# Depthwise convolution: the middle kernel column computed by VectorE and ScalarE instead of TensorE

## The chip, the cores and the metric

The kernel runs on one core of a Trainium2 chip. The metric is the device time of one execution in microseconds (us), lower is better. A core has TensorE (PE; its weight loads are listed as PEld), VectorE (DVE), ScalarE (ACT), GpSimd (POOL) and SyncE (SP, which here only issues DMAs). [...]

## What is computed

The input is a batch of 16 images of 56 x 56 pixels with 384 channels, float32. There are two layers. The first is a group normalisation, a dilated attention over 3 x 3 neighbours with dilations 1, 2 and 3, a projection and a residual sum. The second, which the change touches, is a group normalisation, a depthwise 3 x 3 convolution with weights of -1, 0 or 1, and a residual sum:

```python
def _L1_conv_ref(x, w):
    kh, kw, C, mult = w.shape
    w_clip = jnp.clip(w, -1.0, 1.0)
    binary_kernel = w_clip + lax.stop_gradient(jnp.sign(w_clip) - w_clip)
    k = binary_kernel.reshape(kh, kw, 1, C * mult)
    return lax.conv_general_dilated(x, k, window_strides=(1, 1), padding='SAME', rhs_dilation=(1, 1),
                                    dimension_numbers=('NHWC', 'HWIO', 'NHWC'), feature_group_count=C)
...
x = x + _L0_conv_ref(_gn(x), L0_conv_w_qkv, L0_conv_w_proj, L0_conv_b_proj)
x = x + _L1_conv_ref(_gn(x), L1_conv_w)
```

## The kernel before

An image (in the code a block, `b`) is cut into 7 chunks (`c`) of 8 rows, 448 pixels; 112 chunks (`m`) go through three stages. Channels lie on the partitions in 3 groups (`j`) of 128.

Stage A (`plan_a`) loads a chunk, turns it to channels-first on PE, copies it out of PSUM on ACT (`xa`, L435), takes statistics on DVE (L436) and writes it to DRAM (`xd`). Stage B (`plan_b`) is the attention: projections to keys and values (`pkv`) and to queries (`pq`) at L464 on PE, products `t` of queries and keys on DVE (L517), their sums over channels on PE (`ps`, L502), a softmax on DVE, ACT and POOL (L532 to L563), the weights spread over channels on PE (`pb_a`, L581), their products `w` with the values on DVE (L588), sums of these on POOL (L596 to L600), the output projection (`po`, L614), residual sum and statistics on DVE (L617, L620), and a write to DRAM (`x1d`). Stage C (`plan_c`) is the second layer.

In stage C the channel groups 0 and 1 (`JG` = 2 of 3) are convolved on PE. `load` brings three copies `z` of 32 channels, shifted by one row each, onto 96 partitions, `normalise` scales them on ACT (L698), and `convolve` sums over the three rows of the kernel by a matmul with `kdiag`, a 96 x 32 matrix that holds three diagonals of taps, once for each of the three kernel columns (`kx`) and each of the four sets of 32 channels (`q`). The middle column has the full width of 448, the outer two 440 because the edge pixel drops out. Then DVE adds the sum `pc` in PSUM to the residual `x1` (L719; the profile lists that tile as `x`). The third group is convolved elsewhere: on ACT and POOL (`taps_g`, `sum_g`, L770 to L786), in the last block on DVE (`taps_last`, L754). `turn` transposes the result back on PE (`pt_o`, L793), ACT copies it and a DMA writes it out.

The order of the work is written by hand. `at(when, order, piece)` puts a piece in a time slice, nine slices to a chunk (`STEP`), and the number `order` ranks the pieces of one slice (SOFTMAX, SCORE, WEIGH_AHEAD, BURST, STATISTICS, CONVOLVE, WEIGH, QUERY and so on). The pieces are issued in this order; a scheduler then lays the instructions of each engine out by this priority and by what is ready in its own estimate, so the order on the chip deviates from the list in places. In stage C chunk `m` begins at slice `t0` = 9 (m + 10); its two groups are convolved in slices `t0 + 2` and `t0 + 5` (one later where `c` is 0), the residual is loaded at `t0 - 1` and `turn` runs from `t0 + 9`. The last block has denser slices of its own and borrows buffers from stages that are over.

Buffers that matter: `ps_mt`, three PSUM banks, shared by `pkv`, `pt_x`, `pc`, `po`, `pt_s` and `pt_o`; one PSUM buffer each for `pq`, `ps` and for `pb_a` (three banks wide); two `x1`; three `xa`. Group statistics reach stage C as `mr` (shift and scale of each channel, 128 partitions) and `mrz` (the same on the 96 partitions of `z`), from `spread_out`.

Of the kernel before, what the change touches and what calls it, by code (L numbers as in the profile page):

```python
# [35 lines left out]
def dilated_attention_then_binary_conv(  # L36
# [99 lines left out]

    spread = const.tile([P, 2, P], BF16, name="spread")

    ktap = const.tile([P, NTAP], F32, name="ktap")

    kdiag = const.tile([K3, 3, JG * NQ, HD], F32, name="kdiag")

    xin_p = ctx.enter_context(tc.tile_pool(name="xin_p", bufs=1))
    z_p = ctx.enter_context(tc.tile_pool(name="z_p", bufs=2))
    xa_p = ctx.enter_context(tc.tile_pool(name="xa_p", bufs=3))
    st_p = ctx.enter_context(tc.tile_pool(name="st_p", bufs=2))
    dr_p = ctx.enter_context(tc.tile_pool(name="dr_p", bufs=3, space=DRAM))
    xn_p = ctx.enter_context(tc.tile_pool(name="xn_p", bufs=3))
# [6 lines left out]
    x1_p = ctx.enter_context(tc.tile_pool(name="x1_p", bufs=2))  # L155
    xg_p = ctx.enter_context(tc.tile_pool(name="xg_p", bufs=2))
    m_p = ctx.enter_context(tc.tile_pool(name="m_p", bufs=3))
    o_p = ctx.enter_context(tc.tile_pool(name="o_p", bufs=2))


# [34 lines left out]
    def load_small_weights():  # L195

        raw["small"] = t = m_p.tile([P, 3, PX], F32, tag="m", name="small")
        flat = t.rearrange("p k n -> p (k n)")
        at_ = [0]

        def room(parts, n):
            at_[0] += n
            return flat[:parts, at_[0] - n : at_[0]]

        raw["b"] = room(NG, P)
        raw["k"], raw["kp"] = room(K3, 3 * NG * NQ), room(K3, 3 * NG * NQ)
        raw["kg"] = room(P, NTAP)
# [25 lines left out]
    def small_weights():  # L233
# [27 lines left out]

        binary(raw["kp"], raw["k"])
        kp = raw["kp"].rearrange("p (k s) -> p k s", k=3)
        binary(ktap, raw["kg"])
        eye3 = raw["eye"]
        nc.gpsimd.memset(eye3, 0.0)
        for ky in range(3):
# [4 lines left out]
        for kx in range(3):  # L272
            nc.vector.tensor_tensor(
                kdiag[:, kx],
                kp[:, kx, : JG * NQ].unsqueeze(2).to_broadcast([K3, JG * NQ, HD]),
                eye3.unsqueeze(1).to_broadcast([K3, JG * NQ, HD]),
                ALU.mult,
            )
        raw.clear()

    def rows(ap):
        return ap.rearrange("p (r w) -> p r w", w=W)
# [104 lines left out]
    def chunk_of(dram, c):  # L387
        return dram.rearrange("(j p) n -> p j n", p=P)[:, :, c * PX : (c + 1) * PX]
# [7 lines left out]
    stats0, stats1 = {}, {}  # L396
    xd, x1d = {}, {}
    mr0, mr1 = {}, {}
    first = {}
    last_term = {}  # L400

# [44 lines left out]
    def plan_b(m, t0):  # L446
# [198 lines left out]
        for j in range(NG):  # L645
            at(t0 + 24 + j, PROJECT, lambda j=j: out_project(j))

    def plan_c(m, t0):

        b, c = divmod(m, NCH)  # L650
# [38 lines left out]
        def normalise(j):  # L689
# [9 lines left out]
            for edge in edges(j):  # L699
                nc.gpsimd.memset(edge, 0.0)  # L700

        def load_x():
            had["x1"] = x1 = x1_p.tile([P, JG, PX], F32, tag="x1", name="x1")
            nc.sync.dma_start(x1, chunk_of(x1d[b], c)[:, :JG])  # L704

        def convolve(j):
            pc = ps_mt.tile([P, 512], F32, tag="mt", name="pc")
            pcr = rows(pc[:, :PX])

            def tap(kx, q):  # L710
                lo, hi = max(0, 1 - kx), W - max(0, kx - 1)
                return nc.tensor.matmul(  # L712
                    pcr[q * HD : (q + 1) * HD, :, lo:hi], kdiag[:, kx, j * NQ + q, :],
                    rows(set_of(j, q))[:, :, lo + kx - 1 : hi + kx - 1], start=(kx == 1), stop=(kx == 2),
                )
# [3 lines left out]
            nc.vector.tensor_tensor(x1[:, j], pc[:, :PX], x1[:, j], ALU.add)  # L719

        lo, hi = (0 if c else 1), ROWS + (2 if c < NCH - 1 else 1)
        zp = zg[m % 2]

        def load_g():
# [21 lines left out]
        def taps_last(ky):  # L746

            mid = had["xg"][:, 1 : ROWS + 1, :]
            if ky == 0:
                had["m"] = m_p.tile([P, 3, PX], F32, tag="m", name="m")  # L750
            acc = rows(had["m"][:, 0])
            for kx in range(3):
                o = 3 * ky + kx
                nc.vector.scalar_tensor_tensor(  # L754
                    mid if o == 8 else acc, zp[:, ky : ky + ROWS, kx : kx + W], ktap[:, o : o + 1],
                    acc if o else mid, op0=ALU.mult, op1=ALU.add,
                )

# [7 lines left out]
        def taps_g(ky):  # L766
            t = m_p.tile([P, 3, PX], F32, tag="m", name="m")
            for kx in range(3):
                o = 3 * ky + kx
                nc.scalar.activation(  # L770
                    rows(t[:, kx]), zp[:, ky : ky + ROWS, kx : kx + W], AF.Copy, scale=ktap[:, o : o + 1]
                )
# [15 lines left out]
        def turn(s):  # L788
            pt = ps_mt.tile([P, 512], F32, tag="mt", name="pt_o")
            mid = had["xg"][:, 1 : ROWS + 1, :].rearrange("p r w -> p (r w)")  # L790
            for j in range(NG):
                src = mid if j == JG else had["x1"][:, j]
# [10 lines left out]
        if b == B - 1:  # L803
# [54 lines left out]
    def statistics(when, sets):  # L858
# [3 lines left out]
        def norm(k, *which):  # L862
            if not steps:
                steps["of"] = group_norm([
                    (stats1[b], lambda mr, mrz, b=b: mr1.update({b: (mr, mrz)}), True) if layer
                    else (stats0[b], lambda mr, b=b: mr0.update({b: mr}), False)
                    for layer, b in sets
                ])
            steps["of"][k](*which)
# [49 lines left out]
```

## Time and profile before

| quantity | value |
|---|---|
| median of 3 runs | 5223.8 us (5223.65 to 5231.6) |
| the profiled execution | 5223.35 us, its span 5221.6 us |
| mean granted TensorE clock | 0.984 |
| L712, all matmuls of the convolution | 5040 with `z` in, 336 with `z_last` (the last block) |
| L588, `w` on DVE | 1008, 1560.3 us busy |
| L517, `t` on DVE | 1008, 1528.6 us busy |
| L596, sums of `w` on POOL | 672, 2048.7 us busy |
| L770, taps of the third group on ACT | 945, 658 ns each |
| DVE waiting for `pc` at L719 | 239.3 us |
| PE waiting for `w` at `pb_a` | 36.7 us |
| DMA, mean | 158 GB/s, 825.62 MB |

A line of groups reads: line of the code, engine, operation, output <- input, shapes, count, then busy time, mean length of one in ns, and the idle time of that engine right before it with what ended it. A line of the timeline reads: start, length, engine, line, operation, and in brackets the idle time before it. A float32 matmul appears as two records in the trace. Times in the text that look like 2083.95 are microseconds from the start of the span.

### The profile page before, as it was taken

To read this page: it belongs to the slowest core of one execution; us is meant where nothing else is said; L and a number is where in the kernel's file an instruction comes from. 1 tells how busy PE (TensorE), PEld (TensorE's weight loads), DVE (VectorE), ACT (ScalarE), POOL (GpSimd) and SP (SyncE) were. 2 spreads that over 40 slices of the span, in tenths; PEclk is the share of its full clock that TensorE was granted. 3 is DMA by queue.
4 is the path that set the end of the run, shared out by engine and by line. 5 is a ranking of instruction groups with operands and counts; after the bars stand their busy time and mean duration, and the time that the engine had idled before them with its cause. 6 is when DMAs were issued, how large, how long until landed. Compare 5 with 4: busy or idle time off the path is not lost. (4 is left out here: it accounts for less than half of the span.)

```text
span 5221.6 us, 75614 instructions
## 1 busy us (share of the span) xinstructions
PE 5085.7 (97%) x26885; PEld 2322.5 (44%) x26885; DVE 4199.0 (80%) x4125; ACT 2310.7 (44%) x4077; POOL 4242.2 (81%) x2950
## 2 busy tenths in 40 slices
PE   8999999999999999999999999999999999999976
PEld 4444444444444444444444444444444444444433
DVE  4898888888888888888888888888888888878764
ACT  3223444444444544444444444444445444444444
POOL 2677878888888888889888888888888888888881
PEclk8999999999999999999999999999999999999987
DMA  6444656666566565656666565665666656554445
GB/s 197 127 124 119 167 160 166 163 166 167 162 169 165 161 163 159 168 158 166 166 166 165 163 166 162 165 163 160 164 163 171 167 163 168 141 138 135 121 135 158
DMA packets 811631, 825.62 MB, mean 158 GB/s; under 512 B 360307, under 2 KB 801014, under 8 KB 811254
## 3 DMA queue, kind: packets, MB, share of 16 engines
q1 hardware_dynamic: 803270, 808.79, 56.9%
q10 hardware_dynamic: 7984, 12.00, 0.7%
q8 instruction: 213, 3.49, 0.3%
q14 instruction: 164, 1.34, 0.1%
HBM read 466.41 MB, written 231.21 MB: 134 GB/s over the span
## 5 line engine op out<-in xcount | busy, mean ns | idle before, releaser
L596 POOL TENSOR_TENSOR w<-w 128x1344 f32<-128x1344 f32 x672 | 2048.7, 3049 | 327.3 <-DVE w L588 279.1
L517 DVE TENSOR_TENSOR t<-pq,k 128x1344 f32<-128x1344 f32 x1008 | 1528.6, 1550 | 237.8 <-PE pq L464 236.6
L588 DVE TENSOR_TENSOR w<-pb_a,v 128x1344 f32<-128x1344 f32 x1008 | 1560.3, 1548 | 172.6 <-PE pb_a L581 91.9
L464 PE MATMUL pkv<-xn,wqkvT 128*128 128x448 f32 x3924 | 1542.2, 542 | 3.9 <-ACT xa L435 3.5
L464 PEld LDWEIGHTS pkv<-xn,wqkvT 128*128 128x128 f32 x3924 | 725.9, 190 | 664.7 <-issue 634.7
L614 PE MATMUL po<-y,wprojT 128*128 128x448 f32 x2016 | 834.9, 550 | 17.3 <-POOL y L600 17.3
L464 PE MATMUL pq<-xn,wqkvT 128*128 128x448 f32 x1962 | 834.9, 560 | 0.0
L698 ACT ACTIVATE z<-z,mrz 96x448 f32<-96x448 f32 x840 | 573.9, 751 | 266.0 <-DMA z<-x1d 239.7
L777 POOL TENSOR_TENSOR m<-m 128x1344 f32<-128x1344 f32 x210 | 639.1, 3044 | 43.3 <-ACT m L770 37.9
L502 PE MATMUL ps<-t,sel 128*32 128x448 f32 x6048 | 660.8, 546 | 0.3 <-DVE t L517 0.2
L474 ACT COPY v<-pkv 128x448 f32<-128x448 f32 x336 | 178.1, 530 | 918.3 <-PE pkv L464 911.1
L770 ACT ACTIVATE m<-zg,ktap 128x448 f32<-128x448 f32 x945 | 552.6, 658 | 15.1 <-POOL m L777 5.7
L614 PEld LDWEIGHTS po<-y,wprojT 128*128 128x128 f32 x2016 | 376.1, 191 | 374.1 <-issue 347.1
L712 PE MATMUL pc<-z,kdiag 96*32 96x440 f32 (+1 forms) x5040 | 519.3, 545 | 7.1 <-POOL z L700 4.3
L464 PEld LDWEIGHTS pq<-xn,wqkvT 128*128 128x128 f32 x1962 | 345.2, 190 | 318.8 <-issue 318.8
L617 DVE SCALAR_TENSOR_TENSOR xr<-po,bias,xr 128x448 f32<-128x448 f32 x336 | 227.9, 678 | 277.8 <-PE po L614 272.7
L435 ACT COPY xa<-pt_x 128x448 f32<-128x448 f32 x315 | 167.4, 534 | 618.2 <-PE pt_x L423 618.2
L558 POOL TENSOR_TENSOR rest<-ew,e 112x512 f32<-112x512 f32 x112 | 130.1, 1162 | 358.9 <-ACT e L554 358.9
L581 PE MATMUL pb_a<-aT,spread 24*128 24x448 bf16 x3024 | 369.5, 360 | 42.7 <-DVE w L588 36.7
L600 POOL TENSOR_TENSOR y<-y,w 128x448 f32<-128x448 f32 x336 | 381.7, 1136 | 23.8
L599 POOL TENSOR_TENSOR y<-w 128x448 f32<-128x448 f32 x336 | 382.8, 1139 | 19.3
L581 PEld LDWEIGHTS <-spread 24*128 24x128 bf16 x3024 | 100.8, 91 | 621.4 <-issue 603.6
(132 smaller groups left out, 4307.6 us busy)
## 6 DMA issues: line engine op xcount, KB each, us to landing
z<-x1d SPq DMA_DIRECT2D x570, 224.0 KB, 4.0
xr<-xd SPq DMA_DIRECT2D x112, 672.0 KB, 4.3
x1d<-xr SPq DMA_DIRECT2D x112, 672.0 KB, 3.2
xn<-xd SPq DMA_DIRECT2D x109, 672.0 KB, 4.5
xin<-in_x_dram SPq DMA_DIRECT2D x105, 672.0 KB, 7.3
xd<-xa SPq DMA_DIRECT2D x315, 224.0 KB, 3.2
out_dram<-osb SPq DMA_DIRECT2D x420, 168.0 KB, 3.4
x<-x1d SPq DMA_DIRECT2D x112, 448.0 KB, 8.5
```

What stands on the lines that cost most here:

```text
L464: nc.tensor.matmul(dst[:, :PX], wqkvT[:, cc, o0 : o0 + P], had["xn"][:, cc, :], start=(cc == 0), stop=(cc == NG - 1))
L502: return nc.tensor.matmul(had["ps"][32 * j : 32 * j + 32, :PX], sel[:, s0 : s0 + 32], tk, start=(issued[j] == 1), stop=(issued[j] == len(r ...
L517: nc.vector.tensor_tensor(t.rearrange("p k (r w) -> p k r w", w=W), q3, k3, ALU.mult)
L581: return nc.tensor.matmul(pb[:, kx, :PX].rearrange("p (s n) -> p s n", s=NSUB), spread[rows_of, v % 2, :], had["a"][rows_of, :, v // 8, :] ...
L588: nc.vector.tensor_tensor(w.rearrange("p k (r w) -> p k r w", w=W), pb[:, :, :PX].rearrange("p k (r w) -> p k r w", w=W), three(kv[1][g][m ...
L596: nc.gpsimd.tensor_tensor(w0, w0, w, ALU.add)
L599: nc.gpsimd.tensor_tensor(y, w0[:, 0], w0[:, 1], ALU.add)
L614: nc.tensor.matmul(po[:, :PX], wprojT[:, g, j * P : (j + 1) * P], had[f"y{g}"], start=(g == 0), stop=(g == NG - 1))
L698: nc.scalar.activation(z, z, AF.Identity, bias=mrz[:, j, q, 0:1], scale=mrz[:, j, q, 1:2])
L712: return nc.tensor.matmul(pcr[q * HD : (q + 1) * HD, :, lo:hi], kdiag[:, kx, j * NQ + q, :], rows(set_of(j, q))[:, :, lo + kx - 1 : hi + k ...
L770: nc.scalar.activation(rows(t[:, kx]), zp[:, ky : ky + ROWS, kx : kx + W], AF.Copy, scale=ktap[:, o : o + 1])
L777: nc.gpsimd.tensor_tensor(had["m"], had["m"], t, ALU.add)
```

## The change

The middle column (`kx` = 1) of the groups 0 and 1 is no longer a matmul. With the normalisation of a channel written as scale and shift, its three taps act on the raw residual `x1`: above, centre and below, each times (tap x scale), plus a constant (sum of the taps in range x shift). `column_scalars` computes these factors once a block on POOL, adding 1 to the centre's so that the residual sum is in it. For each group `column` computes the centre and the constant on ACT into a new buffer `u` (one, of 448 elements), in the first or last chunk of an image in two instructions, because the border row has another constant. In `convolve` PE adds up the two outer columns, DVE then adds the taps above and below into `pc` in PSUM by two multiply-adds, and the last add takes `u` in place of `x1`.

`load_x` brings ten rows in place of eight and is placed at `t0 - 4`, ahead of `load(0)` in that slice. `column` is placed in the slice of its `convolve`, at the rank STATISTICS, ahead of CONVOLVE; in the last block it has the rank CONVOLVE itself. At the start the taps of all three groups are loaded to `ktap` by three DMAs in place of one. `xa` has two buffers in place of three, and the small tile `sm` of the softmax shares the buffer of `mx`. The three buffers of `m_p`, which hold the last block's products, are as before.

```diff
-    xa_p = ctx.enter_context(tc.tile_pool(name="xa_p", bufs=3))
+    xa_p = ctx.enter_context(tc.tile_pool(name="xa_p", bufs=2))
...
+    u_p = ctx.enter_context(tc.tile_pool(name="u_p", bufs=1))
...
-        nc.sync.dma_start(raw["kg"], w_conv.rearrange("y x c m -> c (y x m)")[JG * P : (JG + 1) * P, :])
+        for j in range(NG):
+            nc.sync.dma_start(
+                raw["kg"][:, j * NTAP : (j + 1) * NTAP],
+                w_conv.rearrange("y x c m -> c (y x m)")[j * P : (j + 1) * P, :],
+            )
...
+        up, mid, down = (ktap[:, :JG, o] for o in (1, 4, 7))
+        nc.vector.tensor_add(kcol[:, :, 0], mid, down)
+        nc.vector.tensor_add(kcol[:, :, 1], kcol[:, :, 0], up)
+        nc.vector.tensor_add(kcol[:, :, 2], up, mid)
...
-            sm = s_p.tile([SUB, NSUB, GH], F32, tag="sm", name="sm")
+            sm = s_p.tile([SUB, NSUB, GH], F32, tag="mx", name="sm")
...
+    def column_scalars(b):
+
+        mr = mr1[b][0]
+        cs = st_p.tile([P, JG, 6], F32, tag="cs", name="cs")
+        nc.gpsimd.tensor_tensor(
+            cs[:, :, 0:3], ktap[:, :JG, 1:NTAP:3], mr[:, :JG, 1:2].to_broadcast([P, JG, 3]), ALU.mult
+        )
+        nc.gpsimd.tensor_tensor(cs[:, :, 3:6], kcol, mr[:, :JG, 0:1].to_broadcast([P, JG, 3]), ALU.mult)
+        nc.gpsimd.tensor_scalar(cs[:, :, 1], cs[:, :, 1], 1.0, None, op0=ALU.add)
+        cs1[b] = cs
...
         def load_x():
-            had["x1"] = x1 = x1_p.tile([P, JG, PX], F32, tag="x1", name="x1")
-            nc.sync.dma_start(x1, chunk_of(x1d[b], c)[:, :JG])
+            had["x1"] = x1 = x1_p.tile([P, JG, ROWS + 2, W], F32, tag="x1", name="x1")
+            nc.sync.dma_start(
+                x1[:, :, lo:hi, :].rearrange("p j r w -> p j (r w)"),
+                x1d[b].rearrange("(j p) n -> p j n", p=P)[:, :JG, p0 + (lo - 1) * W : p0 + (hi - 1) * W],
+            )
+
+        def column(j):
+
+            x1, cs = had["x1"], cs1[b]
+            had["u"] = u = u_p.tile([P, ROWS, W], F32, tag="u", name="u")
+            parts = [(0, 1, 3), (1, ROWS, 4)] if c == 0 else [(0, ROWS, 4)]
+            if c == NCH - 1:
+                parts = [(0, ROWS - 1, 4), (ROWS - 1, ROWS, 5)]
+            for r0, r1, of in parts:
+                nc.scalar.activation(
+                    u[:, r0:r1], x1[:, j, r0 + 1 : r1 + 1], AF.Identity, bias=cs[:, j, of : of + 1], scale=cs[:, j, 1:2]
+                )
...
-            in_one_go([lambda kx=kx, q=q: tap(kx, q) for kx in (1, 0, 2) for q in (3, 0, 1, 2)])
-            x1 = had["x1"]
-            nc.vector.tensor_tensor(x1[:, j], pc[:, :PX], x1[:, j], ALU.add)
+            in_one_go([lambda kx=kx, q=q: tap(kx, q) for kx in (0, 2) for q in (3, 0, 1, 2)])
+            x1 = had["x1"][:, j]
+            mid = x1[:, 1 : ROWS + 1]
+            cs, above, below = cs1[b], 1 if c == 0 else 0, ROWS - 1 if c == NCH - 1 else ROWS
+            nc.vector.scalar_tensor_tensor(
+                pcr[:, above:], x1[:, above:ROWS], cs[:, j, 0:1], pcr[:, above:], op0=ALU.mult, op1=ALU.add
+            )
+            nc.vector.scalar_tensor_tensor(
+                pcr[:, :below], x1[:, 2 : below + 2], cs[:, j, 2:3], pcr[:, :below], op0=ALU.mult, op1=ALU.add
+            )
+            nc.vector.tensor_tensor(mid, pcr, had["u"], ALU.add)
...
+                at(t0 + 1 + j, CONVOLVE, lambda j=j: column(j))
                 at(t0 + 1 + j, CONVOLVE, lambda j=j: convolve(j))
...
-        at(t0 - 1, LOADS, load_x)
+        at(t0 - 4, LOADS, load_x)
         for j in range(JG):
             at(t0 - 4 + 3 * j, LOADS, lambda j=j: load(j))
+            at(t0 + 2 + 3 * j + late, STATISTICS, lambda j=j: column(j))
             at(t0 - 1 + 3 * j + late, NORM, lambda j=j: normalise(j))
             at(t0 + 2 + 3 * j + late, CONVOLVE, lambda j=j: convolve(j))
```

More of the change, by code (lines that the diff above doesn't have):

```diff
@@ L137, in dilated_attention_then_binary_conv @@
     spread = const.tile([P, 2, P], BF16, name="spread")
-    ktap = const.tile([P, NTAP], F32, name="ktap")
-    kdiag = const.tile([K3, 3, JG * NQ, HD], F32, name="kdiag")
+    ktap = const.tile([P, NG, NTAP], F32, name="ktap")
+    kcol = const.tile([P, JG, 3], F32, name="kcol")
+    kdiag = const.tile([K3, 2, JG * NQ, HD], F32, name="kdiag")
     xin_p = ctx.enter_context(tc.tile_pool(name="xin_p", bufs=1))
     z_p = ctx.enter_context(tc.tile_pool(name="z_p", bufs=2))
-    xa_p = ctx.enter_context(tc.tile_pool(name="xa_p", bufs=3))
+    xa_p = ctx.enter_context(tc.tile_pool(name="xa_p", bufs=2))
     st_p = ctx.enter_context(tc.tile_pool(name="st_p", bufs=2))
@@ L206, in load_small_weights @@
         raw["k"], raw["kp"] = room(K3, 3 * NG * NQ), room(K3, 3 * NG * NQ)
-        raw["kg"] = room(P, NTAP)
+        raw["kg"] = room(P, NG * NTAP)
         raw["eye"] = room(K3, HD)
@@ L263, in small_weights @@
         kp = raw["kp"].rearrange("p (k s) -> p k s", k=3)
-        binary(ktap, raw["kg"])
+        binary(ktap.rearrange("p j o -> p (j o)"), raw["kg"])
+        up, mid, down = (ktap[:, :JG, o] for o in (1, 4, 7))
+        nc.vector.tensor_add(kcol[:, :, 0], mid, down)
+        nc.vector.tensor_add(kcol[:, :, 1], kcol[:, :, 0], up)
+        nc.vector.tensor_add(kcol[:, :, 2], up, mid)
         eye3 = raw["eye"]
@@ L271, in small_weights @@
             )
-        for kx in range(3):
+        for kx in (0, 2):
             nc.vector.tensor_tensor(
-                kdiag[:, kx],
+                kdiag[:, kx // 2],
                 kp[:, kx, : JG * NQ].unsqueeze(2).to_broadcast([K3, JG * NQ, HD]),
@@ L398, in dilated_attention_then_binary_conv @@
     mr0, mr1 = {}, {}
+    cs1 = {}
     first = {}
@@ L700, in normalise @@
                 nc.gpsimd.memset(edge, 0.0)
+        lo, hi = (0 if c else 1), ROWS + (2 if c < NCH - 1 else 1)
         def load_x():
-            had["x1"] = x1 = x1_p.tile([P, JG, PX], F32, tag="x1", name="x1")
-            nc.sync.dma_start(x1, chunk_of(x1d[b], c)[:, :JG])
+            had["x1"] = x1 = x1_p.tile([P, JG, ROWS + 2, W], F32, tag="x1", name="x1")
[13 more added lines that the diff above has]
+                )
         def convolve(j):
@@ L710, in tap @@
             def tap(kx, q):
-                lo, hi = max(0, 1 - kx), W - max(0, kx - 1)
+                x0, x1 = max(0, 1 - kx), W - max(0, kx - 1)
                 return nc.tensor.matmul(
-                    pcr[q * HD : (q + 1) * HD, :, lo:hi], kdiag[:, kx, j * NQ + q, :],
-                    rows(set_of(j, q))[:, :, lo + kx - 1 : hi + kx - 1], start=(kx == 1), stop=(kx == 2),
-                )
-            in_one_go([lambda kx=kx, q=q: tap(kx, q) for kx in (1, 0, 2) for q in (3, 0, 1, 2)])
-            x1 = had["x1"]
-            nc.vector.tensor_tensor(x1[:, j], pc[:, :PX], x1[:, j], ALU.add)
-        lo, hi = (0 if c else 1), ROWS + (2 if c < NCH - 1 else 1)
+                    pcr[q * HD : (q + 1) * HD, :, x0:x1], kdiag[:, kx // 2, j * NQ + q, :],
+                    rows(set_of(j, q))[:, :, x0 + kx - 1 : x1 + kx - 1], start=(kx == 0), stop=(kx == 2),
+                    skip_group_check=True,
+                )
+            in_one_go([lambda kx=kx, q=q: tap(kx, q) for kx in (0, 2) for q in (3, 0, 1, 2)])
[9 more added lines that the diff above has]
+            nc.vector.tensor_tensor(mid, pcr, had["u"], ALU.add)
         zp = zg[m % 2]
@@ L754, in taps_last @@
                 nc.vector.scalar_tensor_tensor(
-                    mid if o == 8 else acc, zp[:, ky : ky + ROWS, kx : kx + W], ktap[:, o : o + 1],
+                    mid if o == 8 else acc, zp[:, ky : ky + ROWS, kx : kx + W], ktap[:, JG, o : o + 1],
                     acc if o else mid, op0=ALU.mult, op1=ALU.add,
@@ L770, in taps_g @@
                 nc.scalar.activation(
-                    rows(t[:, kx]), zp[:, ky : ky + ROWS, kx : kx + W], AF.Copy, scale=ktap[:, o : o + 1]
+                    rows(t[:, kx]), zp[:, ky : ky + ROWS, kx : kx + W], AF.Copy, scale=ktap[:, JG, o : o + 1]
                 )
@@ L791, in turn @@
             for j in range(NG):
-                src = mid if j == JG else had["x1"][:, j]
+                src = mid if j == JG else had["x1"][:, j, 1 : ROWS + 1].rearrange("p r w -> p (r w)")
                 nc.tensor.transpose(pt[:SUB, j * P : (j + 1) * P], src[:, s * SUB : (s + 1) * SUB], ident)
@@ L864, in norm @@
                 steps["of"] = group_norm([
-                    (stats1[b], lambda mr, mrz, b=b: mr1.update({b: (mr, mrz)}), True) if layer
+                    (stats1[b], lambda mr, mrz, b=b: (mr1.update({b: (mr, mrz)}), column_scalars(b)), True) if layer
                     else (stats0[b], lambda mr, b=b: mr0.update({b: mr}), False)
```

## The prediction

> **What bounds the kernel now.** I read the page's table of busy time first, then the busy time by stretches, then the groups of instructions by shape, and last one chunk in order of time on TensorE (PE) and VectorE (DVE).
>
> ```profile
> PE 5085.7 (97%) x26885; PEld 2322.5 (44%) x26885; DVE 4199.0 (80%) x4125; ACT 2310.7 (44%) x4077; POOL 4242.2 (81%) x2950
> 200.00:400.00 200.00, 200.00 (x867) 88.25 (x866) 181.05 (x169) 44.28 (x79) 145.17 (x89) 1.00 0.47 133
> 500.00:4800.00 4300.00, 4272.47 (x22833) 1945.47 (x22831) 3538.65 (x3413) 2001.25 (x3533) 3660.72 (x2414) 1.00 0.60 162
> ```
>
> In the second and third line the columns are the stretch, its length, then busy time of PE, PEld, DVE, ACT, POOL, the granted clock, DMA share and GB/s. From 500 to 4800 us PE is idle for 27.5 us in 4300, at full clock: PE is the bound, and any PE time taken out can be gained until somebody else is late. DVE is busy 82%, POOL 85%, ACT 47%. The stretch from 200 to 400 us, before any convolution runs, shows something useful: there DVE is busy 90.5% and PE still never idles.
>
> ```profile
> L712 PE MATMUL pc<-z,kdiag 96*32 96x440 f32 x3360 | 355.3, 541 | 0.0
> L712 PE MATMUL pc<-z,kdiag 96*32 96x448 f32 x1680 | 202.7, 554 | 7.1 <-POOL z L700 4.3 <-ACT z L698 2.5 <-DVE x L719 0.3
> L719 DVE TENSOR_TENSOR x<-pc,x 128x448 f32<-128x448 f32 x224 | 139.4, 622 | 241.6 <-PE pc L712 239.3 <-DMA x<-x1d 2.3
> L617 DVE SCALAR_TENSOR_TENSOR xr<-po,bias,xr 128x448 f32<-128x448 f32 x336 | 227.9, 678 | 277.8 <-PE po L614 272.7
> ```
>
> The 448-wide row is the middle column, the 440-wide one the two outer ones. L719 empties the convolution today: DVE reaches it early and waits 239.3 us for PE over the run.
>
> ```profile
> 2075.32 0.60 DVE L538 TENSOR_REDUCE mx<-pt_s 112x48 f32<-112x432 f32 x1
> ...
> 2082.42 1.53 DVE L588 TENSOR_TENSOR w<-pb_a,v 128x1344 f32<-128x1344 f32 x1
> 2084.38 0.62 DVE L719 TENSOR_TENSOR x<-pc,x 128x448 f32<-128x448 f32 x1 [0.43 <-PE pc L712]
> 2084.92 1.55 DVE L588 TENSOR_TENSOR w<-pb_a,v 128x1344 f32<-128x1344 f32 x1
> 2087.10 1.56 DVE L517 TENSOR_TENSOR t<-pq,k 128x1344 f32<-128x1344 f32 x1 [0.63 <-PE pq L464]
> ...
> 2090.57 3.00 DVE L517 TENSOR_TENSOR t<-pq,k 128x1344 f32<-128x1344 f32 x2
> ```
>
> ```profile
> 2081.90 2.41 PE L712 MATMUL pc<-z,kdiag 96*32 96x448 f32 x24
> 2084.25 0.36 PE L581 MATMUL pb_a<-aT,spread 24*128 24x448 bf16 x3
> 2084.54 2.52 PE L464 MATMUL pq<-xn,wqkvT 128*128 128x448 f32 x6
> 2086.99 0.36 PE L581 MATMUL pb_a<-aT,spread 24*128 24x448 bf16 x3
> ...
> 2093.83 1.71 PE L502 MATMUL ps<-t,sel 128*32 128x448 f32 x16
> ```
>
> This is the tight part of an ordinary chunk: DVE works without a pause from 2071.79 (softmax, products `t`, `w`) to 2083.95, and its only idle time before `t` ends at 2093.57 is 0.43 + 0.63 = 1.06 us. The score burst `ps` starts 0.26 us after that `t`. Later in the chunk DVE waits 2.28 us for `po`.
>
> **What the Trainium skill says.** TensorE: Matmul & The Clock Gate, Part 3 (packing): matmuls whose outputs lie in different 32-partition column tiles run at the same time. The trace agrees: 24 matmuls of about 0.54 us end within 2.41 us. VectorE: DVE Perf Modes, the perf-mode tier table: an fp32 operand in PSUM keeps an operation at one element a cycle; the trace agrees (L588 against L719: 926 ns for 896 more elements, 1.03 ns each). SBUF — State Buffer, Who interferes with whom: a VectorE instruction with two SBUF inputs contends with a GpSimd one that reads SBUF, one with a single SBUF input does not. The trace agrees: L546, two SBUF inputs, takes 0.609 us at the median and 3.362 at most; L617, PSUM and SBUF, never exceeds 0.685. The new multiply-adds are of L617's kind. PSUM — Partial Sum Buffer, The four PSUM rules: the first matmul of a group clears written-marks for its bank and quadrants, and a later one overwrites where a mark is clear. So the edge column that only the third tap column writes comes out right without the middle one; no run here shows it yet.
>
> **The change part by part.**
>
> *PE, removed.* One of three tap columns: 8 of the 24 matmuls in 2.44 us (the usual length of L712 in the timeline), 0.81 us a channel group, two groups: 1.63 us a chunk. 105 chunks outside the last block: 171 us. In the last block the clock is about 0.7 and the two groups take 8 us, so 2.7 us a chunk less, which is treated below.
>
> *DVE, added.* Two multiply-adds per group, PSUM and SBUF in, PSUM out. No row of before writes PSUM from DVE. Below: 0.61, the pitch at which an L617 lets the next operation start. Above: if reading and writing the same PSUM tile do not overlap, 0.62 + 448 x 1.03 ns = 1.08, taken as 1.15. I take 0.70, the pitch of the chained multiply-adds of L754 at the end of the run: +1.4 us a group, +2.8 a chunk. The add that remains is today's L719 with `u` for `x1`. DVE goes from 3538.65/96 = 36.9 us a chunk (96 softmaxes in the stretch) to 39.7; PE from 44.5 to 42.9. That is 92.5% of PE, a little above the 90.5% at which PE did not idle.
>
> *What is queued behind them.* The new operations wait for `pc`, with a `w` and a `t` behind them on DVE; `pb_a` has one buffer, so PE waits for that `w`. Keeping the order above: `pc` ends at 2083.5, but PE's next `pb_a` waits for the `w` that ends at 2083.95, and `pq` behind it ends at 2086.7. DVE is free at 2083.95 too: the three convolution steps end at 2085.95, the next `w` at 2087.4. So PE stands until 2087.4 at the `pb_a` that was at 2086.99: 0.4 late instead of 0.81 early, and `ps` with it (its `t` ends at 2093.57 - 1.06 + 1.4 = 2093.9 and does not hold it longer). The second group (`pc` at 2095.76) then gives its 0.81 back, and DVE catches up in the pause before `po`. By this walk only 0.4 us of 1.63 remain a chunk. Against it: the order is laid out again for the new costs, and PE has projections ready that need nothing of DVE; 200 to 400 us shows that it finds them. I let an ordinary chunk give back 0.33 us (about a quarter of the walk's 1.23), bounds 0 and 1.23.
>
> *Chunks with statistics*, 15 in the steady part: DVE has 2.6 us more there (L345, 2.63 at the median, behind a POOL sum), and already stalls PE by 1.42 us at 2007.95. I take 1.1 of 1.63 given back, bounds 0 and 2.5.
>
> *ScalarE.* `column`: 224 activations like L770 at 0.66, 150 us over the run; ACT reaches 50%. It waits for `x1`, which is asked for three slices sooner, and stands ahead of its matmuls; 0. Without that cover (x1 late) evictions of `pkv` queue behind it; the DMA lands in 8.5 us and six slices of about 5 us are left. Bounds 0 and 0.2 a chunk.
>
> *POOL.* Three small operations a block, about 0.2 us each: 10 us over the run, plus a wait for `mr` with sums behind it. 0, bounds 0 and 1 us a block.
>
> *SP and DMA.* `load_x` takes ten rows for eight, 112 KB more a chunk (12.5 MB on 825.6), and passes ahead of the first `z` load on SP; already today it is issued at 2096.66, before `z` at 2098.26. ACT waits 239.7 us for `z` in all, but that `z` is multiplied some 12 us later. 0, bounds 0 and 0.3. Two `xa` buffers for three: a turn every two slices, landing 3.2 us: 0. The shared softmax tag: `mx` is read out before `sm` is written: 0.
>
> *Start.* Two more tap loads of 1152 small elements (today's one landed in 10.6 us, while DMA is full to 40 us) and some small DVE operations: +3 us, bounds 0 and 10.
>
> *Last block.* About 13.4 us a chunk. DVE is in the ring: L719 at 5185.79, six tap sums to 5190.52, `z_last`, and PE starts at 5191.12. PE loses 2.7 us a chunk; DVE, 8.5 us of work in it, gains 2.8 and ends later behind each `pc`. Taken as 0, bounds -12 and +12 for seven chunks.
>
> *Sum.* -171 + 90 x 0.33 (30) + 15 x 1.1 (17) + 3 = -121. From the profiled execution's 5223.35 us (span 5221.6): 5102. The median of the runs shown, 5223.8, is 0.45 us off, nothing here.
>
> **Rivals.**
> A, as summed: 5102, with 0.1 to 0.9 us given back its own range is 5075 to 5155. Chance 0.45.
> B, PE stays full: nothing given back, 5055. For it: 200 to 400 us. Against: DVE at 92.5% and POOL at 38.1/42.9 = 89% together, where POOL had only 73% in that stretch. 0.17.
> C, the walk holds: 90 x 0.4 - 3 = 33 us, 5190. For it: no pause on DVE from 2071.79 to 2083.95. 0.15.
> N, the returns eat just what is saved, within 0.2%: 0.05.
> D, slower: the in-place multiply-adds cost 1.15 us. DVE gains 2.3 us before `w` in each group; in the walk that exceeds its pause of 1.06 plus the 0.81 that comes back later by 0.43. 90 x 0.43 + 15 x 1 + 3 = +57: 5280. It decides from about 0.94 us each on. For it: no row shows DVE writing PSUM. Against: DVE would still have 41.5 us of work for 42.9. 0.18.
> That the computation differs (edge column) would not change the time.
>
> **How the numbers follow.** Forecast 5102. A and B and C are faster: 0.77; same 0.05 (0.2%, about 10 us, is what a measurement of this kernel can tell from no change); slower 0.18. The range leaves out D's upper part and B's lower edge: 5040 to 5230. A's own range stands above.
>
> **What would show it.** Right: PE about 98% in 500 to 4800 with L712 at two thirds of its matmuls; DVE 91 to 93%; the new lines at 0.6 to 0.75 us; more waits of `pb_a` for `w` than today's 36.7 us, some 50. Wrong: multiply-adds over 0.9 us (D); `pb_a` waiting over 100 us (C); PE over 99% (B); ACT waiting for `x1`, or a last block over 10 us longer.

## Result and profile after

| kernel | median (lowest to highest), runs | ratio to before |
|---|---|---|
| before | 5226.58 us (5223.65 to 5231.6), 4 | |
| after | 5152.15 us (5150.29 to 5160.07), 4 | 0.9867, 95% interval 0.9855 to 0.9879 |

The change makes the kernel 1.3% faster. The forecast was 5102 us, 121 us below the profiled execution of before. The profiled execution of after took 5160.07 us, 63 below it; it is the slowest of its four, and by the medians the change gives 74. So between a half and two thirds of what was forecast arrived. The rest of this text asks where the other part is.

First the page's table of busy time of the kernel after, then its stretch from 500 to 4700 us (columns as in the prediction: stretch, length, busy time of PE, PEld, DVE, ACT and POOL, clock, DMA share, GB/s):

```profile
PE 4967.5 (96%) x25093; PEld 2259.1 (44%) x25093; DVE 4475.9 (87%) x4575; ACT 2478.8 (48%) x4365; POOL 4248.0 (82%) x2998
```

```profile
500.00:4700.00 4200.00, 4143.10 (x21157) 1881.54 (x21157) 3749.61 (x3774) 2126.96 (x3747) 3639.68 (x2437) 1.00 0.61 167
```

PE is still the bound, with 56.9 us of pauses in 4200 (1.35%; 0.6% before), and DVE is busy 89%, where 91 to 93 was forecast. It has more to do, but the chunk is longer than forecast. The groups by shape of the kernel after:

```profile
L762 DVE SCALAR_TENSOR_TENSOR pc<-x,cs,pc 128x448 f32<-128x448 f32 x192 | 131.9, 687 | 119.5 <-PE pc L752 93.1 <-issue 15.6 <-DMA x<-x1d 4.9
L765 DVE SCALAR_TENSOR_TENSOR pc<-x,cs,pc 128x448 f32<-128x448 f32 x192 | 131.0, 683 | 2.8
L768 DVE TENSOR_TENSOR x<-pc,u 128x448 f32<-128x448 f32 x224 | 137.7, 615 | 2.0 <-ACT u L742 0.2
L752 PE MATMUL pc<-z,kdiag 96*32 96x440 f32 x3360 | 359.5, 546 | 8.8 <-POOL z L723 7.6 <-ACT z L721 0.6 <-ACT osb L846 0.5
```

The first two lines are the new multiply-adds, 0.687 and 0.683 us each, never over 0.691; 0.70 was taken. The last line is what is left of the convolution on PE, 3360 of 5040 matmul records.

To see where the time went, take the sum of the softmax (L544 before, L556 after), which DVE computes once in each chunk; the distance from one to the next is the length of a chunk. Such marks, read from the timelines of both kernels, divide the span:

| stretch | before, us | after, us | difference |
|---|---|---|---|
| start to the 11th softmax sum (no convolution yet) | 507.5 | 515.5 | +8.0 |
| 11th to 101st | 4037.9 | 3963.5 | -74.5 |
| 101st to the last (112th) | 487.2 | 493.0 | +5.8 |
| last one to the end (the last block's convolution) | 189.0 | 186.0 | -3.1 |

Within an image an ordinary chunk goes from 44.1 to 43.4 us. The chunk with the statistics goes from 48.3 to 46.8, the one after it from 44.9 to 43.4, the next mostly from 44.1 to 44.1.

So the steady part gains only 0.7 us in an ordinary chunk. On the timeline of PE, `pc` at L752 keeps PE for 0.75 us less in each group (1.66 for 2.41), 1.5 us a chunk in all. About half of that is lost again inside the chunk. The timeline of PE in the kernel before, with the projections behind the transposes:

```profile
2087.29 0.60 PE L423 MATMUL pt_x<-ident,xin 112*128 112x112 f32 x4
2087.73 0.39 PE L793 MATMUL pt_o<-ident,x 128*112 128x128 f32 x2
2087.95 0.27 PE L793 MATMUL pt_o<-ident,xg 128*112 128x128 f32 x1
2088.06 4.68 PE L464 MATMUL pkv<-xn,wqkvT 128*128 128x448 f32 x12
```

and the same place in the kernel after:

```profile
2541.78 1.66 PE L752 MATMUL pc<-z,kdiag 96*32 96x440 f32 x16
...
2546.42 0.60 PE L435 MATMUL pt_x<-ident,xin 112*128 112x112 f32 x4
2546.86 0.38 PE L841 MATMUL pt_o<-ident,x 128*112 128x128 f32 x2
2547.08 0.27 PE L841 MATMUL pt_o<-ident,xg 128*112 128x128 f32 x1
2547.64 4.78 PE L476 MATMUL pkv<-xn,wqkvT 128*128 128x448 f32 x12 [0.29 <-ACT xa L447]
```

Before, the first `pkv` starts 0.11 us behind the last transpose; after, 0.56 us, behind a wait for ACT's eviction of `pt_x` into `xa`. A projection needs no `xa`. What it needs is a bank: `pc`, `pt_x`, `pt_o` and `pkv` share the three banks of `ps_mt`. The timeline of DVE in the same stretch of after shows who holds one:

```profile
2543.51 0.69 DVE L762 SCALAR_TENSOR_TENSOR pc<-x,cs,pc 128x448 f32<-128x448 f32 x1 [1.00 <-PE pc L752]
2544.11 1.55 DVE L600 TENSOR_TENSOR w<-pb_a,v 128x1344 f32<-128x1344 f32 x1
2545.57 0.68 DVE L765 SCALAR_TENSOR_TENSOR pc<-x,cs,pc 128x448 f32<-128x448 f32 x1
2546.23 1.56 DVE L529 TENSOR_TENSOR t<-pq,k 128x1344 f32<-128x1344 f32 x1
2547.70 0.61 DVE L768 TENSOR_TENSOR x<-pc,u 128x448 f32<-128x448 f32 x1
```

DVE now has three operations on `pc`, and between them stand a `w` and a `t`. So `pc` keeps its bank from 2541.78 to 2548.31, 6.5 us; before it was 3.1 us, from 2081.90 to 2085.00. When PE comes to `pkv`, the bank of `pc` is not free and `pt_o` has only just been written; by the releaser, it gets the bank of `pt_x`. The evictions of `pt_x` by ACT in these two places, before and after, agree:

```profile
2087.93 0.53 ACT L435 COPY xa<-pt_x 128x448 f32<-128x448 f32 x1 [4.90 <-PE pt_x L423]
2547.06 0.53 ACT L447 COPY xa<-pt_x 128x448 f32<-128x448 f32 x1 [5.72 <-PE pt_x L435]
```

Before, `pkv` starts 0.40 us ahead of the end of this eviction (2088.46), so it had the other bank, that of `pc`, free since 2085.00. After, it starts 0.05 us behind that end (2547.59), with `pc` still to be emptied until 2548.31.

The waits of the whole run, kernel after (waiting engine and line, releaser, then us in all, times, the longest):

```profile
PE pb_a L593 <- DVE w L600: 48.4, 47, 2.5
PE pkv L476 <- ACT xa L447: 26.2, 78, 3.5
PEld pkv L476 <- ACT xa L447: 45.8, 78, 4.2
```

and of the kernel before:

```profile
PE pb_a L581 <- DVE w L588: 36.7, 31, 2.4
PEld pkv L464 <- ACT xa L435: 6.4, 12, 0.5
PE pkv L464 <- ACT xa L435: 3.5, 12, 0.3
```

The wait that the prediction watched, `pb_a` for `w`, grew by 11.7 us over the run, and the wait of `pkv` for `xa` went from 12 places to 78. These are my two theories. The first is **the held bank**: the added work costs nothing as such, and the time is lost because `pc` keeps one of three banks for twice as long. Its rival is **the load**: DVE has 2.8 us more to do in a chunk, `w` comes later for it, and PE waits at `pb_a` or for what follows.

### The profile page after: what moved, and what is told of

Same layout as the page of the kernel before. It is cut to its first block, busy times and chain, and to the rows that moved or that the text cites. A ratio compares the mean times of both kernels' runs of the same rounds, so it can differ in the third digit from the quotient of the medians.

```text
span 5157.9 us, 72661 instructions
## 1 busy us (share of the span) xinstructions
PE 4967.5 (96%) x25093; PEld 2259.1 (44%) x25093; DVE 4475.9 (87%) x4575; ACT 2478.8 (48%) x4365; POOL 4248.0 (82%) x2998
## 5 line engine op out<-in xcount | busy, mean ns | idle before, releaser
L476 PE MATMUL pq<-xn,wqkvT 128*128 128x448 f32 x1962 | 862.4, 567 | 0.0
L818 ACT ACTIVATE m<-zg,ktap 128x448 f32<-128x448 f32 x945 | 568.9, 659 | 17.6 <-POOL m L825 8.5
L593 PE MATMUL pb_a<-aT,spread 24*128 24x448 bf16 x3024 | 370.4, 360 | 52.6 <-DVE w L600 48.4
L629 DVE SCALAR_TENSOR_TENSOR xr<-po,bias,xr 128x448 f32<-128x448 f32 x336 | 227.5, 677 | 210.7 <-PE po L626 205.8
L752 PE MATMUL pc<-z,kdiag 96*32 96x440 f32 x3360 | 359.5, 546 | 8.8 <-POOL z L723 7.6
```

The source lines that it names most:

```text
L476: nc.tensor.matmul(dst[:, :PX], wqkvT[:, cc, o0 : o0 + P], had["xn"][:, cc, :], start=(cc == 0), stop=(cc == NG - 1))
L593: return nc.tensor.matmul(pb[:, kx, :PX].rearrange("p (s n) -> p s n", s=NSUB), spread[rows_of, v % 2, :], had["a"][rows_of, :, v // 8, :] ...
L752: return nc.tensor.matmul(pcr[q * HD : (q + 1) * HD, :, x0:x1], kdiag[:, kx // 2, j * NQ + q, :], rows(set_of(j, q))[:, :, x0 + kx - 1 : x ...
L818: nc.scalar.activation(rows(t[:, kx]), zp[:, ky : ky + ROWS, kx : kx + W], AF.Copy, scale=ktap[:, JG, o : o + 1])
```

## The experiments

All ratios are to the kernel before on the same chip, with a 95% interval. The lengths of chunks and the stretches are those of the profiled execution.

**One part of the change at a time.** `pe_only` leaves out the three taps of the middle column altogether:

```diff
-            nc.vector.scalar_tensor_tensor(
-                pcr[:, above:], x1[:, above:ROWS], cs[:, j, 0:1], pcr[:, above:], op0=ALU.mult, op1=ALU.add
-            )
...
-            nc.vector.tensor_tensor(mid, pcr, had["u"], ALU.add)
+            nc.vector.tensor_tensor(mid, pcr, mid, ALU.add)
...
-            at(t0 + 2 + 3 * j + late, STATISTICS, lambda j=j: column(j))
```

> Leaves out all three taps of the middle kernel column (no u, no multiply-adds; the last add takes x1), so that only the PE part of the change remains. Bank theory (the new kernel keeps only half of the PE time it saves because pc stays in one of the three shared PSUM banks for 6.5 us a group instead of 3.1): pc is short-lived again, so the whole saving shows, 1.52 us a chunk, an ordinary chunk of 42.6 us and 5065 to 5080 us in all. Load theory (VectorE is 89% busy and late with w): the same, since its work is gone too. If the chunk stays near 43.4 us, PE itself loses the time and both theories fall.

Measured: 5111.9 us, ratio 0.9791 (0.9776 to 0.9805), ordinary chunk 42.8 us: 32 us above the range that both theories had set, and 0.2 above their chunk. Where these 0.2 are is seen below, side by side with the others. `dve_only` is the other part alone: all the added work of DVE, ACT and POOL, with the middle column left on PE as well (by the first column's taps) and so counted in two places:

```diff
-                    rows(set_of(j, q))[:, :, x0 + kx - 1 : x1 + kx - 1], start=(kx == 0), stop=(kx == 2),
+                    rows(set_of(j, q))[:, :, x0 + kx - 1 : x1 + kx - 1], start=(kx == 1), stop=(kx == 2),
...
-            in_one_go([lambda kx=kx, q=q: tap(kx, q) for kx in (0, 2) for q in (3, 0, 1, 2)])
+            in_one_go([lambda kx=kx, q=q: tap(kx, q) for kx in (1, 0, 2) for q in (3, 0, 1, 2)])
```

> Puts the middle column back on PE beside the new work on VectorE and ScalarE (that column is counted twice, with the first column's taps). If what is given back is a fixed price of the new work, the two parts add up: this run less before equals the new kernel less the one with the PE part alone, about +75 to +85 us, 5300 us. If the new work hides behind a longer PE, it is 5230 to 5250, of which about 8 at the start. Bank theory: PE waits of pkv for the eviction of xa about as many as in the new kernel (78). Load theory: fewer waits of any kind than in the new kernel.

Measured: 5281.5 us, 1.0115 (1.01 to 1.013), ordinary chunk 44.7, 0.6 above before; the total lies between the two ranges of the expectation. The two parts nearly add up: the ordinary chunk loses 1.3 us by the one and gains 0.6 by the other, and 0.7 net is what after shows. Both theories can live with that. But the waits of `dve_only` lean to the bank:

```profile
PEld pkv L476 <- ACT xa L447: 44.8, 78, 3.5
PE pb_a L593 <- DVE w L600: 33.5, 29, 2.5
PE pkv L476 <- ACT xa L447: 25.2, 78, 2.7
```

With all the added work of DVE, PE waits no more for `w` than before (36.7 us in 31 places), and for the bank as often as in after.

**The bank freed sooner.** `add_first` keeps all the work. It only issues the next `t` on DVE behind the addition that frees `pc`:

```diff
+    def behind_add(what):
+        if what not in add_of[1]:
+            return nullcontext()
+        add_of[1].discard(what)
+        return tc.issue_after(add_of[0].ins)
...
-            nc.vector.tensor_tensor(t.rearrange("p k (r w) -> p k r w", w=W), q3, k3, ALU.mult)
+            with behind_add("t"):
+                nc.vector.tensor_tensor(t.rearrange("p k (r w) -> p k r w", w=W), q3, k3, ALU.mult)
...
-            nc.vector.tensor_tensor(mid, pcr, had["u"], ALU.add)
+            add_of[0] = nc.vector.tensor_tensor(mid, pcr, had["u"], ALU.add)
+            add_of[1] = {"w", "t"}
```

> Only the order on VectorE: the next score product t is issued behind the add that frees pc, instead of between the second multiply-add and that add. Bank theory: pc of the first group is free some 1.5 us sooner, pkv no longer waits for xa (0.45 us a chunk, 78 waits), an ordinary chunk falls from 43.4 to about 42.9, 5110 to 5125 us in all. Load theory: VectorE has the same work, chunk 43.4, 5145 to 5160.

Measured: 5093.27 us, 0.9754 (0.9739 to 0.9768), some 58 us below after and 17 below the range of the bank theory, ordinary chunk 42.7. `pkv` waits for `xa` in 13 places, where it was 78 in after. DVE in the timeline of `add_first`:

```profile
2518.31 0.69 DVE L771 SCALAR_TENSOR_TENSOR pc<-x,cs,pc 128x448 f32<-128x448 f32 x1 [0.21 <-PE pc L761]
2518.91 1.55 DVE L609 TENSOR_TENSOR w<-pb_a,v 128x1344 f32<-128x1344 f32 x1
2520.38 0.68 DVE L774 SCALAR_TENSOR_TENSOR pc<-x,cs,pc 128x448 f32<-128x448 f32 x1
2521.09 0.62 DVE L777 TENSOR_TENSOR x<-pc,u 128x448 f32<-128x448 f32 x1
```

and PE:

```profile
2516.58 1.66 PE L761 MATMUL pc<-z,kdiag 96*32 96x440 f32 x16
...
2521.88 0.27 PE L851 MATMUL pt_o<-ident,xg 128*112 128x128 f32 x1
2521.99 4.68 PE L484 MATMUL pkv<-xn,wqkvT 128*128 128x448 f32 x12
```

The addition ends at 2521.71, before the last transpose, and `pkv` starts 0.11 us behind that transpose again, without a wait. All of DVE's added work is still there, and its busy share from 500 to 4700 us rises to 91%. With all of it the kernel is faster than `pe_only`, which does none of it. So the load is not what after loses. (`pe_only` is no lower bound, because leaving operations out also lays the order out anew: there PE waits 59.2 us at `pb_a` for `w`, here 37.0.)

**The same wait brought into the kernel before.** `hold_before` takes the kernel before, with no work added, and puts the addition behind the next `t` (the last eleven chunks keep the old order):

```diff
-            nc.vector.tensor_tensor(t.rearrange("p k (r w) -> p k r w", w=W), q3, k3, ALU.mult)
+            product = nc.vector.tensor_tensor(t.rearrange("p k (r w) -> p k r w", w=W), q3, k3, ALU.mult)
...
+            if late_add:
+                with tc.issue_after(product.ins):
+                    late_add.pop()()
...
-            nc.vector.tensor_tensor(x1[:, j], pc[:, :PX], x1[:, j], ALU.add)
+            late_add.append(lambda: nc.vector.tensor_tensor(x1[:, j], pc[:, :PX], x1[:, j], ALU.add))
+            if b == B - 1 or m > N - 12:
+                late_add.pop()()
```

> The kernel before the change, with the one addition that frees the bank of pc issued behind the next score product t; no work added or taken away. If it is the time for which pc keeps its bank that costs, the projections wait for the eviction into xa in some 78 places, an ordinary chunk goes from 44.1 to 44.6 us or so, and the time is 5255 to 5275. If it is VectorE's added work, this order costs nothing: 5221, chunk 44.1.

Measured: 5294.36 us, 1.0136 (1.0122 to 1.015), ordinary chunk 44.7, the length of `dve_only` without any of its work. PE in the timeline of `hold_before`:

```profile
2481.65 0.27 PE L799 MATMUL pt_o<-ident,xg 128*112 128x128 f32 x1
2482.21 4.78 PE L465 MATMUL pkv<-xn,wqkvT 128*128 128x448 f32 x12 [0.29 <-ACT xa L436]
```

It is the picture of after to the hundredth: 0.56 us from transpose to projection, 0.29 of it the wait for `xa`. `pkv` waits for `xa` in 65 places and for `osb`, the eviction of `pt_o`, in 14 more. DVE in the same stretch:

```profile
2480.80 1.56 DVE L518 TENSOR_TENSOR t<-pq,k 128x1344 f32<-128x1344 f32 x1 [0.81 <-PE pq L465]
2484.27 0.61 DVE L723 TENSOR_TENSOR x<-pc,x 128x448 f32<-128x448 f32 x1
```

`pc` was complete at 2478.01. DVE stands for 0.81 us ahead of this `t` and does not take the addition in the meantime: it keeps the order of its queue, in which a `w` and a statistics operation follow before the addition.

The total is 19 us above the expected range, since the chunks with statistics became 49.4, 51.1 or 52.8 us long (48.3 before), where I had expected an ordinary chunk's loss. In those of 51.1 us the granted clock is at half once for 3.4 us, in those of 52.8 twice, in those of 49.4 never; the last section comes back to that.

The smaller number of `xa` buffers is not why `pkv` waits for `xa`: `hold_before` has three of them, and the kernel before with two (`before_xa2`, below) waits in 12 places, as before.

**The order alone, and the work with the order.** Two controls: `before_add_first` is the kernel before with `t` behind its addition, `dve_first` is `dve_only` with it. Both edits are those of `add_first`.

> The kernel before the change with the next score product t behind the addition that frees the bank, nothing else. There pc keeps its bank for 3.1 us already: the order has little to give, 5215 to 5223 us and a chunk of 44.1. If the order is worth something for itself, whatever the change does, the kernel before gains as much as the changed one did from it (57 us): about 5165.

Measured: 5223.88 us, 1.0 (0.9991 to 1.0009), ordinary chunk 44.1. This control says less than it was meant to: between the 21st and the 101st softmax sum of the kernel before, no `t` stands between a complete `pc` and its addition in any of the 160 groups, so there the edit had nothing to move.

> The kernel dve_only (all three columns on TensorE, the middle one counted twice over by the added VectorE and ScalarE work) with the next score product t behind the addition that frees the bank. If the held bank is the whole of what the added work costs, an ordinary chunk is back at 44.1 to 44.2 us and the time at 5221 to 5230 (5 us of it from the start). If VectorE's added 2.8 us a chunk cost something for themselves, the chunk stays above 44.4 and the time above 5245.

Measured: 5254.56 us, 1.0059 (1.0042 to 1.0076): in time on the side of the load, though the ordinary chunk is 44.3 us, just over the bank's 44.2. The stretches show why. Against before it has +9.1 us up to the 11th softmax sum, +14.6 in the 90 chunks of the steady part (`dve_only`: +42.6), -5.5 up to the last sum, and +15.9 from there to the end. The last is the block whose convolution nothing else covers: with all three columns on PE the added work does cost time there, 15 us in `dve_only` too. I had left it out of this expectation.

Side by side, with the time from the first matmul of `pc` to the end of the addition, read for the first and the second group of an ordinary chunk:

| kernel | `pc` in its bank, us | added DVE work | conv. columns on PE | places where `pkv` waits for `xa` | ordinary chunk, us |
|---|---|---|---|---|---|
| before | 3.1, 3.1 | no | 3 | 12 | 44.1 |
| `before_add_first` | 3.1, 3.1 | no | 3 | 12 | 44.1 |
| `dve_first` | 5.9, 5.9 | yes | 3 | 13 | 44.3 |
| `dve_only` | 7.3, 7.3 | yes | 3 | 78 | 44.7 |
| `hold_before` | 9.3, 7.3 | no | 3 | 65, and 14 for `osb` | 44.7 |
| `add_first` | 5.1, 4.3 | yes | 2 | 13 | 42.7 |
| `pe_only` | 2.4, 2.4 | no | 2 | 12 | 42.8 |
| after | 6.5, 5.2 | yes | 2 | 78 | 43.4 |

Within each half the chunk is long where `pkv` waits, and it makes no difference whether DVE has the added work. The hold alone does not set the length: 5.9 us in `dve_first` still end before `pkv` comes, 6.5 in after do not.

The 0.1 or 0.2 us that are left can be placed too. The next table divides PE's time in an ordinary chunk by tile, each counted from its first record to the first record of the next tile (my sums from the traces, mean of 33 ordinary chunks). A wait ahead of `pkv` so falls to the `pt_o` in front of it. The tiles left out differ by at most 0.02 us.

| us in a chunk | before | `dve_first` | `dve_only` | `hold_before` | `add_first` | `pe_only` | after |
|---|---|---|---|---|---|---|---|
| `pc` | 4.72 | 4.72 | 4.71 | 4.71 | 3.10 | 3.21 | 3.23 |
| `pt_o` | 1.65 | 1.65 | 2.10 | 2.10 | 1.65 | 1.65 | 2.10 |
| `pkv` | 13.54 | 13.53 | 13.64 | 13.64 | 13.64 | 13.53 | 13.64 |
| `pq` | 7.17 | 7.37 | 7.17 | 7.17 | 7.27 | 7.37 | 7.37 |

The wait for the bank is the same 0.45 us in all three kernels that have it, and `pkv` takes 0.10 more in them (as it does in `add_first`). These 0.55 us are the whole loss of `hold_before` and of `dve_only`. The further 0.20 at `pq` in after, `dve_first` and `pe_only` is there because a `pb_a` stands inside one of its `pq` in the order laid out for these kernels (2 and 4 records in place of 6). `pe_only` has none of the added work, so the 0.2 us of `dve_first` do not speak for the load. In an ordinary chunk no run shows a cost of DVE's added work itself.

**The start.** The first softmax sum lies at 102.7 us before and at 107.7 after. Two parts of the change touch the start: three loads of taps that gather single values in place of one, and two `xa` in place of three. `taps_late` issues the three loads in a later slice:

```diff
-        for j in range(NG):
-            nc.sync.dma_start(
...
+    for j in range(NG):
+        at(1, LOADS, lambda j=j: load_column_taps(j))
```

> The three loads of taps by channel are issued after the first image is in, instead of ahead of its last chunks. If the 5 us by which the first softmax comes later (107.7 against 102.7) are theirs, it comes back to 103 and the run is 5144 to 5148. If the start is late for another reason, 5150 to 5154.

Measured: 5150.2 us, 0.9866 (0.9849 to 0.9882), first sum at 107.0. It tells nothing: the scheduler still issued these loads, at 26.3 us, ahead of a part of the image, asked for at 32.8, that PE then waits for (1.97 us at 40.26). `turned` therefore changes the load itself. On top of `add_first` it brings the taps in as nine rows and turns them on PE:

```diff
-        for j in range(NG):
-            nc.sync.dma_start(
-                raw["kg"][:, j * NTAP : (j + 1) * NTAP],
-                w_conv.rearrange("y x c m -> c (y x m)")[j * P : (j + 1) * P, :],
-            )
+        nc.sync.dma_start(raw["rows"], w_conv.rearrange("y x c m -> (y x) (c m)"))
...
+        for j in range(NG):
+            nc.tensor.transpose(
+                pk[:, j * NTAP : (j + 1) * NTAP], raw["rows"][:, j * P : (j + 1) * P], ident[:NTAP, :NTAP]
+            )
+        nc.vector.tensor_copy(raw["kg"], pk[:, : NG * NTAP])
```

> The kernel add_first, with the column's taps brought in at the start as one piece of nine rows of 384 values and turned on TensorE, in place of three transfers that gather single values. If these three transfers make the start late (first softmax sum at 107.6 us in add_first, 102.7 before the change), the first softmax sum comes back to 103 or less and the time is 5085 to 5089 us. If the smaller number of xa buffers makes the start late, the first sum stays at 107 to 108 and the time at 5093.

Measured: 5087.78 us, 0.974 (0.9727 to 0.9754), first sum at 103.1. PE's wait for the image in `add_first`:

```profile
54.41 1.73 PE L443 MATMUL pt_x<-ident,xin 112*128 112x112 f32 x8 [7.27 <-DMA xin<-in_x_dram]
```

and in `turned`:

```profile
49.42 1.73 PE L446 MATMUL pt_x<-ident,xin 112*128 112x112 f32 x8 [4.34 <-DMA xin<-in_x_dram]
```

These loads made the first softmax sum late. Most of this does not last: the 11th sum lies at 512.5 us in `turned`, 513.8 in `add_first` and 507.5 before, so of the 4.5 us that the first sum gained 1.3 are left. What else makes this stretch long stays open. The whole run is 5.5 us shorter by the medians, but the two intervals overlap and the two profiled spans differ by 0.5 us only (5088.4 and 5087.9), so the first sum is shown and a gain at the end is not.

> The kernel before the change with two xa buffers in place of three, nothing else. The prediction put the buffer at nothing: then 5221 us and the first softmax sum at 102.7. If the missing buffer makes the start late, the sum moves to about 107 and the time to 5225 to 5229.

The edit is `bufs=3` to `bufs=2` for `xa_p` in the kernel before. Measured: 5221.69 us, 0.9998 (0.999 to 1.0006), first sum at 101.9. In the kernel before, the third `xa` buffer was worth nothing.

**The early load of x1.** `loadx` puts `load_x` of the kernel after back to its old slice:

```diff
-        at(t0 - 4, LOADS, load_x)
+        at(t0 - 1, LOADS, load_x)
```

> The changed kernel with the load of the first x slice back at its old slice number, one before the block's beginning in place of four before. The prediction put that move at nothing: then 5150 us, as the changed kernel. If the early load gets in the way of the other transfers on SP's queue, some 5 us less; if the column's centre term needs it early, u waits for the load and the time is over 5155.

Measured: 5163.02 us, 0.9885 (0.9872 to 0.9899). Its median is 11 us above after, in the range set for a late `u`, and `u` does wait for the load in 70 places (113.0 us of ACT) in place of 13 (20.9 us). But the intervals of the ratios overlap, the steady part is 3963.4 us against 3963.5, and the profiled spans are 5157.7 and 5157.9: in the steady part these waits of ACT cost nothing. Whether the early load saves a few microseconds elsewhere stays open.

## Why the prediction was right in direction and off in size

**Right.** The result lies in the likeliest case's own range of 5075 to 5155, near its upper end. PE is still the bound and DVE's work is hidden; `add_first` shows it with all of that work at a chunk of 42.7 us. The multiply-adds took 0.683 to 0.687 us for the 0.70 of the prediction, so its slower case (1.15 us each) fell by the row that it named. No run shows a cost of ACT, POOL, SP or the smaller `xa`; ACT did wait for `x1`, as one of the signs of being wrong had it, but by 20.9 us only. The waits of `pb_a` for `w` came out at 48.4 us for "some 50". The last block came out at -3.1 us where nothing was taken; that two opposite effects cancel there is not shown, since it is -2.8 in `pe_only` and +14.8 in `dve_only`. The chunks around the statistics gave 3.0 us in three (137.3 to 134.3), where the prediction's terms make 3.1.

**The step that failed: "I let an ordinary chunk give back 0.33 us".** It gives back 0.75 of 1.49: 0.55 at the bank and 0.20 at the split `pq`. That this lies inside the bounds of 0 and 1.23 is luck, because the bounds come from another wait. The number was made from one walk, in which a late `w` keeps PE at `pb_a`, and then cut to a quarter because PE "has projections ready that need nothing of DVE". That sentence is what the runs refute: the projections need a bank that DVE empties. The walk did not show it for a reason worth noting. It set the three operations on `pc` one behind the other, ending at 2085.95; so placed they free the bank well before `pkv` at 2088.06. On the chip a `w` and a `t` stand between them. I had said that these two are queued behind the new operations, and asked only who waits for `w`, not who waits for the bank while DVE is busy with others. In the 90 steady chunks this cost some 31 us against the forecast (0.6 us in four chunks of every seven).

**Terms that were mis-sized.** PE's saving: 2.44 us was divided by three columns (0.81 a group), while the timeline shows 0.75: 24 records take 2.41 us and 16 take 1.66, so 0.09 for each and some 0.16 for a burst that do not go away with its records (an estimate from these two). In all groups outside the last block L712 and L752 differ by 159.8 us for the 171. The start: +3 was taken, +5.0 came at the first softmax sum and +8.0 by the 11th, inside its bounds of 0 and 10; the loads that it named delay the first sum, but by `turned` only some 1.3 us of the delay at the 11th go with them.

**What was not in it.** The chunks from the 101st to the last, where stage A is over, were treated like the others. They should have become some 14 us shorter (eleven times 1.3) and became 5.8 us longer; these 20 us, the 31 above and the 5 at the start are the most of what is missing. PE in the timeline of after shows such a place:

```profile
4569.77 1.71 PE L514 MATMUL ps<-t,sel 128*32 128x448 f32 x16
4573.11 0.37 PE L593 MATMUL pb_a<-aT,spread 24*128 24x448 bf16 x3 [1.64 <-DVE w L600]
4573.41 2.05 PE L752 MATMUL pc<-z,kdiag 96*32 96x440 f32 x16
4575.39 1.86 PE L476 MATMUL pq<-xn,wqkvT 128*128 128x448 f32 x2
```

DVE, in the same stretch:

```profile
4569.55 2.04 DVE L558 TENSOR_TENSOR ew<-ew,sm 112x432 f32<-112x432 f32 x1
4571.52 1.54 DVE L600 TENSOR_TENSOR w<-pb_a,v 128x1344 f32<-128x1344 f32 x1
```

Here it is the prediction's own mechanism. Without transposes of stage A to fill in, PE stands 1.64 us at `pb_a` for a `w` behind a softmax multiply of 2.04 us (it took 0.61 at 2539.66); then a `pq` of two records takes 1.86 us, where in the steady part it takes 1.02. In the whole stretch PE stands 24.4 us, 14.3 before, and the mean granted clock is 0.962, 0.982 before; length times what is missing to 1 makes 18.7 and 8.8 us lost to the clock. So of the 20 us about half are pauses and half the clock (an estimate from these four figures). `add_first` takes 472.9 us for this stretch in place of 493.0. I read the cause from the timeline; no run was made for it alone.

## What to carry to other kernels

When an accumulator in PSUM gets more steps before it is emptied, price the time that it holds its bank, from the first matmul to the end of the last read, with everything that stands in between in the queue of the engine that empties it, and ask which other matmuls draw on the same banks. A short gap that repeats before matmuls whose data is ready, released by an eviction of some other tile, is its sign: here it was 0.29 us in a chunk. Of the repeating gap the Trainium skill says, under Perfetto Trace Analysis, Optimization Strategy, that on the engine that should be saturated it can mean too little SBUF or PSUM for the next tile; here the gap goes when the bank comes free sooner (78 waits in after, 13 in `add_first`). Then try the order before the work: moving one operation behind the addition that frees the bank was worth 58 us, where the whole change without it was worth 74.

## What the hardware showed beyond that

A multiply-add on DVE that reads and writes the same PSUM tile (0.687 us for 448 columns) costs about the same as one that goes from PSUM to SBUF (0.677 us, L629).

The granted clock falls after shorter pauses than I had thought. The windows around the pause above, kernel after (stretch, length, PE busy, clock, DMA share, GB/s):

```profile
4571.19:4574.60 3.41, 1.77 (x23) 1.00 0.65 226
4574.60:4581.43 6.83, 6.83 (x20) 0.50 0.30 57
4581.43:4600.00 18.57, 18.57 (x85) 1.00 0.62 153
```

After 1.64 us without a matmul the clock is at half for 6.8 us, although PE works again without a pause. The Trainium skill, TensorE: Matmul & The Clock Gate, Why this matters for your kernels, advises against pauses of more than about 3 us. In this trace less is enough, though not always: of the nine pauses of 1.57 to 2.54 us that PE makes between 4450 and 4900 us in after, six are followed by a mean clock of 0.50 to 0.75 over the next 4 us, and three by full clock. Among the twelve pauses of about 1.41 us at the statistics in the kernel before it fell once, to 0.59. It need not be one pause. In `hold_before` two of 0.62 and 0.61 us, with 0.5 us of work between them, were enough:

```profile
741.57:744.98 3.41, 2.18 (x17) 1.00 0.87 212
744.98:748.39 3.41, 3.40 (x5) 0.50 0.52 150
```

In all twelve traces, between 520 us and the last softmax sum but one, the clock falls 50 times, and each time PE had stood for at least 1.21 us of the 3.41 us right before. That is not sufficient: on the same grid of 3.41 us, 77 stretches with as much idle time were not followed by a fall. What decides there, no run here shows.
